# Layer 0 of a four-layer graph network: an interleaved order for its loop, and the threshold guess in two parts

## The chip, the cores and the metric

The kernel runs on one core of a Trainium2 chip. The metric is the device time in microseconds (us). A core has five engines that run their own instruction streams: TensorE (PE; its weight loads are listed as PEld), VectorE (DVE), ScalarE (ACT), GpSimd (POOL) and SyncE (SP), which issues most DMAs. Each engine works its instructions off in order; an instruction whose input is not ready holds up all that are queued behind it on that engine.

## The reference, cut to what matters

There are 4096 nodes with 256 features and a sparse adjacency `adj` (about one entry in a thousand, and the diagonal). Four layers are added to x one after the other, each on relu(layernorm(x)). The change concerns layer 0 alone:

```python
for n in range(2):
    q, k = Xa @ W1.T @ W2.T, Xa @ W3.T            # 64 features
    probs = softmax(q @ k.T)                      # 4096 x 4096
    # keep the largest probabilities of a row until their sum reaches 0.9
    A = probs * mask
    A = A / A.sum(-1)
    Xf = R @ Xf                                   # R: adj + 1, rows scaled to sum 1
    Xa = A @ Xa
    Z = Z + Xf @ U1[n].T + Xa @ U2[n].T
h = layernorm(X + Z)
```

So each of the two steps needs, for each of 4096 rows, a threshold below which its probabilities are dropped. Layers 1 to 3 (a graph convolution, graph attention, a last convolution) are not touched.

## The kernel before, in words

The rows are cut into 32 blocks of 128 (`NB`, `P`): one block is a tile `e` of 128 rows by 4096 columns. `layer0_step` (L1044) builds the functions of one step n, and `period` (L1467) issues the work of one period, b, in which several blocks are under way at once. The order of VectorE, ScalarE and TensorE is the order of the calls, since the code stands under a manual schedule of these three engines; GpSimd and SyncE are ordered by the framework. A block passes through these functions:

- `logits` (L1054) and `exponentials` (L1075): TensorE computes q times k into PSUM, ScalarE takes exp of it into `e`, with a guessed threshold of the row subtracted (`minus_guesses`), in four operations of 1024 columns; their sums give the row's total.
- the search for the threshold: `evaluate` (L1088) passes over `e` on ScalarE twice, with Sign and with Relu, shifted by the present threshold; the accumulated results are the number of entries above it and the mass above it. Points 0 and 1 use the first 1024 columns, points 2 and 3 all 4096. `aim` (L1105) sets the mass to be cut; `update` (L1142, with `measured` and `stepped`) computes the next threshold in some dozen VectorE operations on 128x1 tiles, each of which needs the one before. `bound` (L1160) does the same after point 3 with about 29 of them, and gives an upper bound `hi`.
- `below` (L1210): VectorE takes the entries under `hi` (4096 wide); `segments` (L1218): sixteen maxima (the eight largest of 256 columns each); `listing` (L1225): eleven operations on these 128 candidates, in turn the eight largest and their removal; `decide` (L1238): eight small operations choose the final threshold; `cut` (L1261) and `drop` (L1269) remove what lies under it from `e` (4096 wide each). `drop` also has three small operations for the row's scale `ra`.
- `flip`, `take`, `attend` (L1299 to L1321): TensorE transposes `e` in 8 chunks, ScalarE copies each from PSUM, TensorE multiplies by the features. `attended` (L1327), `turn` (L1338), `weighted` (L1347), `store_xa`, `store_h`, `next_keys` (L1376) finish the block in step 0: the product with U1 and U2 and the keys of step 1. Products of `weighted` and of `next_keys` share one PSUM slot. `add_heads` adds the block to the sum in step 1.
- diffusion (R times Xf): in step 0, `mark` (L1332) reduces the adjacency's rows, loaded in four pieces, to maxima of groups, four reductions a period on VectorE. From these `listed_columns` lists the columns of the entries in pairs of blocks (20 pairs). In step 1 `reach`, `mix` and `mixed` (L1389 to L1425) gather neighbours with GpSimd's indirect DMAs, sum them on TensorE and add them on VectorE, for d=0 first and d=1 later; `spread` and `finish` end a block in the second half of step 1.

`guess` (L938) computes the first thresholds of all 32 blocks from the moments of the keys: squares in eight groups of 512 nodes on TensorE and VectorE, and then a chain of 16 VectorE operations on 128x32 tiles. It runs once at the end of `front` (L983, which normalizes x and builds keys and queries) and once at the end of `close` (L1573), which finishes block 31 of step 0 and lists 14 pairs of columns. The main loops (L1631 to L1661) run periods -2 to 31 for step 0, and -2 to 33 for step 1; the last six pairs are listed in periods -2 and -1 of step 1.

In a period before the change VectorE's order is: `below`, 16 maxima, `update`(b+1, 2), `listing`, two `mark`, `store_xa`'s addition, `aim` and `update`(b+2, 0), `decide`, `cut`, `bound`(b+1), `update`(b+2, 1), two `mark`, `drop`.

## Time and profile before

| | us |
|---|---|
| median of 3 runs | 3821.71 (3820.54 to 3823.34) |
| the profiled execution | 3814.87 |
| its span | 3812.6 |
| first `below` of step 0 | 175.4 |
| last `below` of step 0 | 1441 |
| first `below` of step 1 | 1590 |
| last `below` of step 1 | 2867 |
| layers 1 to 3 begin, about | 2931 |

The mean granted TensorE clock was 0.839. In step 0 `below` comes every 40.95 us; in step 1 every 40.6 to 40.95 us in the first half and every 41.6 to 43.1 us in the second.

How such a page is read: busy time is given for each engine over the span, and in 40 slices of it (a digit is the busy tenth of a slice). Waits are listed as "engine, tile, line <- the engine, tile and line waited for: us in total, times, the longest". A windows view gives for each stretch its length and the busy time of PE, PEld, DVE, ACT and POOL. A timeline line is: start, duration, engine, line, operation, output <- inputs, shapes, how many, and in brackets the idle time before it and what ended it. L12 is line 12 of the kernel.

### The profile page before, as it was taken

What the parts mean: (1) busy time and instruction counts of PE and PEld (TensorE: products, weight loads), DVE (VectorE), ACT (ScalarE), POOL (GpSimd) and SP (SyncE); (2) the same over time, 40 slices, a digit from 0 to 9 for tenths busy, and PEclk for the clock granted to TensorE, in tenths of its full rate; (3) what the DMA queues carried; (4) which work ended last, traced back from release to release, by engine and by line L of the source; (5) the groups of instructions that cost most, each with busy time, mean ns of one, the idle gap of its engine ahead of it and who ended that gap; (6) DMA issues with size and microseconds to landing.
All of it is one profiled execution on the core that took longest, in us unless ns stands there. A gap on an engine that the chain in (4) does not pass through costs nothing. (4 is left out here: it accounts for less than half of the span.)

```text
span 3812.6 us, 43836 instructions
## 1 busy us (share of the span) xinstructions
PE 2628.0 (69%) x12404; PEld 2015.3 (53%) x12404; DVE 2878.5 (75%) x9339; ACT 2245.8 (59%) x3339; POOL 1332.3 (35%) x1342
## 2 busy tenths in 40 slices
PE   6456776776776767467767767767775657688776
PEld 5244554554554555256656656555654445577644
DVE  3499999999999998788888888888884434588500
ACT  3577777777777761676676676767661311577400
POOL 1000000000000000476666625555563476465276
PEclk8778888888888888688878878888887889789878
DMA  3012122122122121333333322222223455444375
GB/s 101 8 63 69 60 75 69 60 75 70 60 75 69 60 91 32 112 111 92 98 107 93 95 65 75 86 90 76 79 88 103 150 168 158 119 128 130 104 216 166
DMA packets 214105, 357.01 MB, mean 94 GB/s; under 512 B 34136, under 2 KB 147293, under 8 KB 213853
## 3 DMA queue, kind: packets, MB, share of 16 engines
q1 hardware_dynamic: 169356, 237.74, 19.5%
q0 software_dynamic: 43520, 116.14, 11.3%
q8 instruction: 102, 1.67, 0.2%
q14 instruction: 151, 1.23, 0.1%
q10 hardware_dynamic: 976, 0.23, 0.0%
HBM read 290.85 MB, written 63.13 MB: 93 GB/s over the span
## 5 line engine op out<-in xcount | busy, mean ns | idle before, releaser
L1096 ACT ACTIVATE unread<-e,next_pair 128x4096 uint8<-128x4096 f32 (+1 forms) x384 | 1098.5, 2861 | 368.7 <-DVE next_pair L1140 237.1
L1305 PE MATMUL pat<-ident,e 128*128 128x128 f32 x2048 | 374.7, 343 | 750.7 <-DVE ra L1274 628.1
L1305 PEld LDWEIGHTS pat<-ident,e 128*128 128x128 f32 x2048 | 306.7, 178 | 848.5 <-issue 663.2
L1321 PE MATMUL pa<-va,at 128*128 128x256 f32 x2048 | 495.0, 400 | 0.1
L1321 PE MATMUL pa<-h,at 128*128 128x256 f32 x2048 | 461.3, 381 | 0.1
L1321 PEld LDWEIGHTS pa<-va,at 128*128 128x128 f32 x2048 | 409.0, 204 | 79.9 <-issue 22.0
L1223 POOL COPY eighth<-best 128x16 f32<-128x16 f32 x64 | 16.8, 262 | 1181.0 <-DVE full_goal L1147 1180.2
L1321 PEld LDWEIGHTS pa<-h,at 128*128 128x128 f32 x2048 | 384.0, 190 | 85.4 <-issue 37.3
L1312 ACT COPY at<-pat 128x512 f32<-128x512 f32 x512 | 287.2, 589 | 142.4 <-PE pa L1321 80.0
L1080 ACT ACTIVATE e<-pl,minus_guess 128x1024 f32<-128x1024 f32 x256 | 283.2, 1114 | 137.5 <-PE pl L1066 116.3
L833 POOL DMA_INDIRECT vg<-v_d,column x320 | 307.0, 959 | 120.4 <-issue 98.3
L1222 DVE MAX8 best<-near 128x8 f32<-128x256 f32 x1024 | 340.9, 411 | 6.3
L1066 PE MATMUL pl<-kt,qb 64*128 64x512 f32 x1024 | 270.3, 638 | 94.7 <-ACT e L1080 94.7
L848 PE MATMUL acc<-vg,ac 128*128 128x256 f32 x768 | 237.9, 459 | 88.0 <-DMA vg<-v_d,column 75.9
L1265 DVE SCALAR_TENSOR_TENSOR e<-e,end_t 128x4096 f32<-128x4096 f32 x64 | 286.6, 4478 | 0.0
L1214 DVE SCALAR_TENSOR_TENSOR near<-e,end_hi 128x4096 f32<-128x4096 f32 x64 | 286.4, 4476 | 0.0
L1272 DVE MATCH_REPLACE8 e<-drop,e 128x4096 f32<-128x4096 f32 x64 | 282.2, 4409 | 0.0
L833 POOL DMA_INDIRECT vg<-far_d,column x160 | 210.0, 1313 | 129.7 <-DVE near L819 81.2
L1909 PE MATMUL acc<-u,tabg 128*65 128x128 f32 x1536 | 210.0, 293 | 61.9 <-DVE u L1894 51.2
L833 POOL DMA_INDIRECT vg<-mixed_d,column x160 | 207.5, 1297 | 125.9 <-PE pr L852 61.6
L848 PEld LDWEIGHTS acc<-vg,ac 128*128 128x128 f32 x768 | 165.7, 229 | 155.9 <-DMA vg<-v_d,column 105.0
L833 POOL DMA_INDIRECT ac<-in_adjt,adj_row x160 | 211.9, 1324 | 79.0 <-issue 40.4
(535 smaller groups left out, 4602.4 us busy)
## 6 DMA issues: line engine op xcount, KB each, us to landing
adj<-in_adjt SPq DMA_DIRECT2D x128, 512.0 KB
ac<-adjc_d SPq DMA_DIRECT2D x96, 384.0 KB
adjc_d<-ac SPq DMA_DIRECT2D x32, 384.0 KB
v_d<-v SPq DMA_DIRECT2D x64, 128.0 KB
vg<-v_d SPq DMA_DIRECT2D x64, 128.0 KB
targets<-steep_d SPq DMA_DIRECT2D x32, 256.0 KB
vg<-v_d,column POOLq DMA_INDIRECT x320, 3.8
table_d<-tab SPq DMA_DIRECT2D x32, 132.0 KB
```

The costliest lines, as they stand in the source:

```text
L833: nc.gpsimd.indirect_dma_start(out, None, rows, bass.IndirectOffsetOnAxis(ap=index, axis=0))
L848: nc.tensor.matmul(acc, ac[:, k, :], v[:, k, :], start=(k == 0), stop=(k == CHUNKS and not own))
L1066: nc.tensor.matmul(pl[:, r, :], s["qb"][rows], kt[rows, j * 512 : (j + 1) * 512], start=True, stop=True,)
L1080: nc.scalar.activation(s["e"][:, j * 1024 : (j + 1) * 1024], pl.rearrange("p r c -> p (r c)"), AF.Exp, bias=minus_guess[:, b : b + 1], acc ...
L1096: nc.scalar.activation(unread[:, :width], s["e"][:, :width], func, bias=s["at"], scale=-1.0, accum_out=s["signs"] if func == AF.Sign else ...
L1214: nc.vector.scalar_tensor_tensor(near, s["e"], end["hi"][:, b : b + 1], s["e"], op0=ALU.is_lt, op1=ALU.mult, accum_out=s["low"])
L1222: nc.vector.max(best[:, k, :], near[:, k * (N // SEG) : (k + 1) * (N // SEG)])
L1265: nc.vector.scalar_tensor_tensor(s["e"], s["e"], last, s["e"], op0=ALU.is_ge, op1=ALU.mult, accum_out=s["held"])
L1272: nc.vector.match_replace(s["e"][:, ::-1], s["drop"], s["e"][:, ::-1], 0.0)
L1305: nc.tensor.transpose(pt[:, k, :], s["e"][:, c * P : (c + 1) * P], ident)
L1312: nc.scalar.copy(at, s["pt", g])
L1321: nc.tensor.matmul(s["pa"], s["at", g][:, k, :], va[:, c, :D], start=(c == 0), stop=(c == NB - 1))
```

## The change

- `some`, `along` and `beside` are added, and the functions made of small VectorE operations become generators that give way after each operation. `along` issues one operation of each of its lines in turn; `beside` issues one of the others after each operation of the first line.
- `period` is ordered anew. The first transposes and takes of the block before, and Sign of point 3, are issued ahead of `below`. After four maxima come more transposes, takes and Relu of point 3; each further maximum is followed by an operation of `bound`. `listing`, the rest of `bound`, and `aim` with `update` 0 go in turn; so do `decide` and two of the marks; then `update` 1. `update` 2 moves from behind the next period's maxima to the end of its own period, in turn with the operations for `ra`, which leave `drop` and become `kept`.
- On ScalarE, Sign of point 2 comes directly after `update` 1, and Relu of point 2 behind the copies of the keys and of `weighted`.
- In step 0 `attended`, `turn`, `next_keys`, `weighted`, `store_xa` and `store_h` treat block b-1 in period b, where they treated b-2 (`attended` b-1).
- `bound` handles its pair of differences and its pair of sums in one operation each, instead of two; `mark` reduces halves of its columns, eight operations a period instead of four.
- `guess` is a generator in two parts: the first group of 512 nodes (blocks 0 to 3), with a chain of its own, and the other seven groups, with another. The second part is issued after period -2 of the step.
- `front` runs with a lag of six blocks instead of five, and its relu is issued one block earlier.
- `close` lists 10 pairs of columns, after period -2 of step 1 five more are listed, and after period -1 the last five.

The diff, cut to its core (of `period` the removed lines are left out, since the function before is printed above):

```diff
 
+    def some(steps, k):
+
+        for _ in zip(range(k), steps):
+            pass
+
+    def along(*lines):
+
+        lines = [iter(line) for line in lines]
+        while lines:
+            for line in list(lines):
+                try:
+                    next(line)
+                except StopIteration:
+                    lines.remove(line)
+
+    def beside(line, *others):
+
+        for _ in line:
+            for other in others:
+                next(other, None)
+
...
+        for lo, hi in ((0, 1), (1, 8)):
+            for g in range(lo, hi + 1):
...
+            bs = slice(4 * lo, 4 * hi)
+            width = 4 * (hi - lo)
+            mu, v, y, t = (sm.tile([P, NB], F32, name=f"guess_{name}", bufs=1)[:, :width] for name in "mvyt")
+            bits = sm.tile([P, NB], U32, name="guess_bits", bufs=1)[:, :width]
+            nc.vector.tensor_copy(mu, pst[:, bs, 1])
...
+            nc.vector.scalar_tensor_tensor(minus_guesses[n][:, bs], mu, -1.0, v, op0=ALU.mult, op1=ALU.subtract)
+            yield
...
-        LAG = 5
+        LAG = 6
+
+        def relu(b):
+            if b % 4 == 0:
+                group = slice(b, b + 4)
+                nc.vector.scalar_tensor_tensor(
+                    shift[:, group, 0], spread_[:, group, 0], -1.0, scale[:, group, 0], op0=ALU.mult, op1=ALU.mult
+                )
+            nc.scalar.activation(
+                h0[:, b, :], x0[b // 16][:, b % 16, :], AF.Relu, bias=shift[:, b, :], scale=scale[:, b, :]
+            )
+
...
+            if 0 <= o + 1 < NB:
+                relu(o + 1)
...
-        guess(0, pm, qt)
+        guesses = guess(0, pm, qt)
+        next(guesses)
+        return guesses
...
-            pair = s["pair"] = s["next"] if k == 3 else small("pair", 2)
+            pair = s["pair"] = s["next"] if k >= 2 else small("pair", 2)
             low, twice, steep = pair[:, 1:2], small("twice"), small("steep")
             nc.vector.tensor_scalar(twice, s["signs"], float(width), s["at"], op0=ALU.add, op1=ALU.mult)
+            yield
             nc.vector.scalar_tensor_tensor(
                 low, twice, 0.5, s["gap"], op0=ALU.mult, op1=ALU.subtract
             )
+            yield
...
+            yield from stepped(pair[:, 0:1], m, s["at"])
+            s["before"], s["next"] = s["pair"], pair
             s["at"] = pair[:, 0:1]
...
-            for k, (new, old) in enumerate(zip((t, low), s["before"])):
-                nc.vector.tensor_sub(diff[:, k : k + 1], new, old)
-                nc.vector.tensor_add(total[:, k : k + 1], new, old)
+            nc.vector.tensor_sub(diff, s["pair"], s["before"])
+            yield
+            nc.vector.tensor_add(total, s["pair"], s["before"])
+            yield
...
+            s = state[b]
+            nc.vector.match_replace(s["e"][:, ::-1], s["drop"], s["e"][:, ::-1], 0.0)
+
+        def kept(b):
+
             s, col = state[b], slice(b, b + 1)
-            nc.vector.match_replace(s["e"][:, ::-1], s["drop"], s["e"][:, ::-1], 0.0)
             ra = s["ra"] = small("ra")
             nc.vector.scalar_tensor_tensor(
                 ra, end["extra"][:, col], end["t"][:, col], s["held"], op0=ALU.mult, op1=ALU.subtract
             )
...
         def mark(b, qs):
             for q in qs:
-                nc.vector.tensor_reduce(
-                    marks[:, :, q, b], state[b]["adj"][q], AX.X, ALU.max, apply_absolute_value=True
-                )
+                for part in (slice(0, CA // 2), slice(CA // 2, CA)):
+                    nc.vector.tensor_reduce(
+                        marks[:, part, q, b],
+                        state[b]["adj"][q][:, part, :],
+                        AX.X,
+                        ALU.max,
+                        apply_absolute_value=True,
+                    )
+                    yield
...
         def period(b):
 
+            old, cur, mid, new = (0 <= k < NB for k in (b - 1, b, b + 1, b + 2))
+            opened, diffused = old and n == 0, pair(b)
             for d, k in pair(b - 1):
                 if k:
                     spread(d)
                     finish(d)
+            if n == 1 and b in (0, NB // 2):
+                reach(0, b // (NB // 2))
+                reach(1, b // (NB // 2))
+            if cur and n == 0:
+                state[b]["adj"] = load_adj(extra, b)
             if old:
                 flip(b - 1, 0)
                 flip(b - 1, 1)
                 take(b - 1, (0, 1))
+            if mid:
+                evaluate(b + 1, 3, (AF.Sign,))
+            best, order = (segments(b), listing(b)) if cur else (iter(()), iter(()))
+            if cur:
+                below(b)
+                some(best, 4)
             if old:
                 flip(b - 1, 2)
                 flip(b - 1, 3)
+                attend(b - 1, 0)
+                attend(b - 1, 1)
+                take(b - 1, (2, 3))
+            if mid:
+                evaluate(b + 1, 3, (AF.Relu,))
+            ahead = bound(b + 1) if mid else iter(())
+            beside(best, ahead)
             if new:
                 exponentials(b + 2)
             if old:
                 flip(b - 1, 4)
                 flip(b - 1, 5)
+                attend(b - 1, 2)
+                attend(b - 1, 3)
             if new:
                 logits(b + 2, 1)
             if old:
                 take(b - 1, (4, 5))
                 flip(b - 1, 6)
                 flip(b - 1, 7)
+            if new:
+                exponentials(b + 2)
+                evaluate(b + 2, 0)
             if old:
                 attend(b - 1, 4)
                 attend(b - 1, 5)
                 take(b - 1, (6, 7))
+            for d, k in diffused[:1]:
+                mix(d, k)
+            if old:
                 attend(b - 1, 6)
                 attend(b - 1, 7)
+            along(order, ahead, chain(aim(b + 2), update(b + 2, 0)) if new else iter(()))
             if new:
                 evaluate(b + 2, 1)
+            if cur:
+                along(decide(b), mark(b, (0, 1)) if n == 0 else iter(()))
+            if opened:
+                attended(b - 1)
+                turn(b - 1)
+            extras = [add_heads(b - 1)] if old and n == 1 else []
+            extras += [mixed(d, k) for d, k in diffused[:1]]
+            along(update(b + 2, 1) if new else iter(()), chain(*extras))
+            if new:
+                evaluate(b + 2, 2, (AF.Sign,))
+            if opened:
+                next_keys(b - 1)
+                weighted(b - 1, 0)
+            if cur:
+                cut(b)
+            if opened:
+                store_xa(b - 1)
+                weighted(b - 1, 1)
+            if new:
+                evaluate(b + 2, 2, (AF.Relu,))
+            if opened:
+                store_h(b - 1)
             if 0 <= b + 3 < NB:
                 logits(b + 3, 0)
             for d, k in diffused[1:]:
                 mix(d, k)
             if cur:
+                if n == 0:
+                    some(mark(b, (2, 3)), 4)
                 drop(b)
+            extras = [kept(b)] if cur else []
+            extras += [mixed(d, k) for d, k in diffused[1:]]
+            along(update(b + 2, 2) if new else iter(()), chain(*extras))
 
         def close(lists):
-
-
-            def listed(k):
-                for _ in zip(range(k), lists):
-                    pass
 
             last = NB - 1
             qt = e_pool.tile([P, N], F32, name="e")
             for g in range(3):
                 cols = slice(g * 1024, (g + 1) * 1024)
                 nc.sync.dma_start(qt[:, cols], q_d[1][:, cols])
-            listed(1)
+            some(lists, 1)
             pm = ps.tile([P, 2, 512], F32, name="pl").rearrange("p r c -> p (r c)")
-            turn(last - 1)
-            next_keys(last - 1)
             nc.sync.dma_start(qt[:, 3072 : last * P], q_d[1][:, 3072 : last * P])
             for g in range(0, 8, 2):
                 flip(last, g)
@@ -1595,26 +1678,22 @@
                     add_moments(g // 2 - 1, pm)
                 if g < 6:
                     by_node(kt1, g // 2)
-                if g == 0:
-                    weighted(last - 1, 0)
-                    store_xa(last - 1)
-                if g == 2:
-                    weighted(last - 1, 1)
-                    store_h(last - 1)
                 attend(last, g)
                 attend(last, g + 1)
             attended(last)
-            listed(14)
+            some(lists, 10)
             turn(last)
             next_keys(last, qt)
             by_node(kt1, 3)
             weighted(last, 0)
             add_moments(3, pm)
             store_xa(last)
-            guess(1, pm, qt)
+            guesses = guess(1, pm, qt)
+            next(guesses)
             weighted(last, 1)
             store_h(last)
             verify()
+            return guesses
 
         return period, logits, verify, close
 
@@ -1629,16 +1708,18 @@
             for n in range(2):
                 nc.sync.dma_start(wu[i][:, :, 1 - n, :], u[n].rearrange("(c p) m -> p c m", p=P))
         with tc.tile_pool(name="front", bufs=1) as xs, tc.manual_schedule(engines=MANUAL):
-            front(h0, kt0, xs)
+            guesses = front(h0, kt0, xs)
         own = st.enter_context(tc.tile_pool(name="own0", bufs=1))
         adj_pool = st.enter_context(tc.tile_pool(name="adj0", bufs=4))
         with tc.manual_schedule(engines=MANUAL):
             period, logits, verify, close = layer0_step(0, h0, kt0, own, adj_pool)
             logits(0, 0)
-            for b in range(-2, NB):
+            period(-2)
+            some(guesses, 2)
+            for b in range(-1, NB):
                 period(b)
             lists = listed_columns(marks, near, ps)
-            close(lists)
+            guesses = close(lists)
 
     with ExitStack() as st:
         s1 = st.enter_context(tc.tile_pool(name="s1", bufs=1))
@@ -1652,12 +1733,11 @@
             logits(0, 0)
             for b in range(-2, NB + 2):
                 period(b)
-                if b < 0:
-                    for _ in zip(range(8), lists):
-                        pass
+                if b == -2:
+                    some(guesses, 2)
+                    some(lists, 5)
                 if b == -1:
-                    for _ in lists:
-                        pass
+                    some(lists, 99)
             verify()
     layer0.close()
 
```

The generators' other functions (`aim`, `stepped`, `update`, `bound`, `segments`, `listing`, `decide`, `mixed`, `add_heads`) are changed only by a `yield` after each operation.

## Prediction

> **What bounds the kernel now.** I read the page's slices first, to see which engine fills layer 0, then the windows by period, to see whether it is full or only often busy, then the timeline of one period for the pitch (start to start) of its operations, and last the waits and the chain.
>
> ```profile
> DVE  3499999999999998788888888888884434588500
> ACT  3577777777777761676676676767661311577400
> 569.70:610.65 40.95, 28.54 (x134) 21.04 (x134) 38.29 (x125) 30.74 (x39) 0.45 (x3) 0.87 0.22 68
> 2700.00:2742.00 42.00, 30.62 (x140) 24.25 (x140) 35.77 (x128) 29.57 (x37) 23.88 (x22) 0.83 0.27 84
> PE pat L1305 <- DVE ra L1274: 628.1, 61, 16.1
> ACT unread L1096 <- DVE next_pair L1140: 237.1, 50, 8.1
> DVE rdeg L1417 <- PE pr L852: 46.9, 16, 3.2
> DMA 2%; POOL 2%; PE 1%; issue 1%; POOLq 0%; ACT 0%; DVE 0%; ACTq 0%
> ```
>
> The slices: VectorE is the full engine over both steps of layer 0 (nines, then eights). The windows (length, then busy PE, PEld, DVE, ACT, POOL): 38.29 of 40.95 us in step 0 and 35.77 of 42.00 late in step 1, ScalarE about 30. The waits: TensorE and ScalarE wait for VectorE, and VectorE hardly waits, except once per odd period of step 1's first half for the mix (46.9 us over 16). The chain covers 6% of the span only, so I don't use it.
>
> ```profile
> 610.62 0.15 DVE L1173 TENSOR_TENSOR diff<-next_pair 128x1 f32<-128x1 f32 x1
> 610.69 0.15 DVE L1174 TENSOR_TENSOR total<-next_pair 128x1 f32<-128x1 f32 x1
> ...
> 612.06 0.16 DVE L1185 TENSOR_TENSOR by<-square 128x1 f32<-128x1 f32 x1
> 612.26 0.16 DVE L1186 SCALAR_TENSOR_TENSOR by<-power,by 128x1 f32<-128x1 f32 x1
> 612.45 0.16 DVE L1187 SCALAR_TENSOR_TENSOR by<-power,by 128x1 f32<-128x1 f32 x1
> ...
> 617.21 3.71 ACT L1096 ACTIVATE unread<-e,next_pair 128x4096 uint8<-128x4096 f32 x1 [3.75 <-DVE next_pair L1140]
> ...
> 621.04 3.71 ACT L1096 ACTIVATE unread<-e,next_pair 128x4096 uint8<-128x4096 f32 x1
> ...
> 623.91 1.94 PE L1305 MATMUL pat<-ident,e 128*128 128x128 f32 x8 [11.45 <-DVE ra L1274]
> 624.19 4.47 DVE L1214 SCALAR_TENSOR_TENSOR near<-e,end_hi 128x4096 f32<-128x4096 f32 x1
> ...
> 640.81 0.37 ACT L1371 COPY hu<-pu 128x256 f32<-128x256 f32 x1 [1.52 <-PE pu L1351]
> ```
>
> Columns: start, duration, engine, line, operation. Two independent 128x1 operations (L1173, L1174) start 0.07 us apart, three that depend on each other (L1185 to L1187) 0.20 apart. A period has some 75 such chained operations: three `update` at about 1.9, `bound` 5.6, `decide` 1.83, `aim` 0.2, reciprocal sums 0.5, together 13.8 us, most of it latency and not work. The rest of VectorE's period: `below` 4.59, sixteen maxima 5.24, listing 3.79, marks 4.6, the hu addition 0.33, `cut` 4.40, `drop` 4.39: 27.3. Sum 41.1 against the measured period of 40.95.
>
> **What the Trainium skill says.** "VectorE: DVE Perf Modes", section The DRAIN you can't avoid, has the next operation start when the pipe is empty, so that dropping semaphores between chained operations gains nothing. "Perfetto Trace Analysis", section Optimizing Scalar/DVE Operations, gives some 60 ns per VectorE instruction and says the write acknowledgement overlaps the next one. The trace agrees with the second for independent small operations (0.07 pitch, 0.15 duration); the dependent pitch of 0.20 is what a chain pays beyond it, and is what interleaving can hide. "ScalarE: Activation LUTs", section What ACT_TABLE_LOAD costs, prices an ACTIVATE with a pointer bias at about 280 ns + 0.833 ns per element: 3.69 us for 4096, the trace has 3.71. "TensorE: Matmul & The Clock Gate", section Part 1, has TensorE fall to half clock after idling; here two transposes took 1.94 us after 11.45 us idle and 1.04 otherwise.
>
> **The change part by part.** Of each period b I set T=0 where `below`(b) starts; `update` 2 of block b+1 has then just ended.
>
> *VectorE's work.* Chain operations put between maxima, list steps and half marks cost 0.07 instead of 0.20. Maxima with eleven operations of `bound`: 5.24 + 11 x 0.07 = 6.0. Listing together with the rest of `bound` (18), `aim` and `update` 0: 5.9 by walking the order at 0.20 per dependent round. `decide` with four half marks 3.8 (8 x 0.20, 4 x 0.60; a half at 0.60 is an estimate: half of the 1.13 of a whole one, plus half of the 0.07 pitch). `update` 1 1.8 (alone with the turn), the other half marks 2.4, `update` 2 with the sums 2.1. With `below`, `cut`, `drop` and the addition: 35.9. The saving in work is 5 us a period.
>
> *The new waits in step 0.* Before, `update` 2 lay after the maxima, and `bound` came a whole `cut` later: Sign and Relu of the third point (3.83 + 3.88) lay beside marks, `drop`, `below`. Now `update` 2 ends a period, Sign 3 starts 0.18 later, the takes of chunks 2 and 3 stand between it and Relu 3 (to 4.83), so `low` is usable at 4.83 + 3.88 = 8.7. VectorE has done `below` and five maxima by 6.3: it waits 2.4, with the remaining maxima queued behind. Next ScalarE has 8.55 of exponentials A to 10.75, takes, exponentials B to about 14, Sign and Relu 0 at 1024 (2 x 1.26): `aim` and `update` 0 wait three times, together 2.1, with the listing queued behind them. Then Sign 2 goes 26.9 to 30.7 (`update` 1 ends 26.8), and the key copies (0.4) and weighted, which now stand behind Sign 2 and the keys' PSUM slot, come after: TensorE's 1.88 to 33.0, hu's copy 0.37; the addition that stood at 31.2 starts at 33.2 to 33.5: 2.2 of wait with marks and `drop` behind it. Waits 6.7. Period: 35.9 + 6.7 = 42.6; transposes after a longer idle time (1.94 for 1.04) delay the first takes and with them Relu 3 by a few tenths: 42.9. Against 40.95 that is +1.95, times 31: **+60**. The copies 0.4, weighted and Relu 2 (usable 37.2) beyond this lie beside `cut`, marks and `drop`. Bounds: each wait could be 0.7 less if ScalarE gets ahead, or 0.7 more: -1 to +1.3 per period.
>
> *Step 1, first half.* No marks and no hu addition, so the third wait is absent: `update` 1 ends at about 26.2 (`add_heads` waits 0.5 to 2 for the last attend on TensorE), `cut` to 30.6, `drop` to 35.0, Relu 2 usable at 34.1, `update` 2 with sums and the mix of d=1 to 37.5 to 38.8. Taken 38.0 against 40.9: -2.9, times 16: **-46**. Half of it is the 3.2 us wait for the mix of odd periods, which now comes after `drop`, far behind its matmul. *Second half*: the finish adds some five more VectorE operations and ScalarE's spread ahead of the takes; 38.6 against the 42.3 of the spacings of `below`: -3.7, times 16: **-59**. GpSimd, about 33 us of gathers a period, still fits into 38; at 36 it would not by much. SP's stores and gathers of `mixed_d` and `summed_d` are issued in the order of the mixes, which come earlier in the period than before; I cost them at nothing as GpSimd's slack of 5 us covers a late one.
>
> *Guess and front.* The first part treats four blocks instead of 32: one squares step of eight and a shorter TensorE pass, 11.5 us less ahead of the exponentials of block 0 (129.9 to about 118.4). The second part, about 16 us (as the whole guess before), falls on VectorE between `update` 2 of block 0 and its `bound`, where ScalarE's evaluations leave it some 10 of idle time. The norm's relu one block ahead takes 0 to 8 from the front loop, 4 taken. First `below` at 172 to 176 against 175.4: **-5** with period 0's fuller overlap.
>
> *Between the steps.* `close` lists 10 pairs of columns instead of 14 at 2.58 each, so the exponentials of step 1's first block come at 72 us after the last `below` instead of 98. But guess part 2 (16), the other ten pairs (25.8) and the chains then stand in series before the first `below`: 160 after the last one instead of 149; ScalarE's lead returns about 6 in the next period: **+5**, with 15 to either side, since it is the part whose order I could follow least.
>
> Sum: +60 - 46 - 59 - 5 + 5 = -45. On the profiled execution's 3814.87 (span 3812.6 and 2.3 around it) that is 3770; the runs' median lies 6.8 above that execution, so **3777**.
>
> **Rivals.**
>
> *A, the waits are hidden in both steps.* ScalarE gets ahead by its 9 us of slack, and VectorE's work alone sets the period: 36 to 37 in both. For it: ScalarE's 31.5 us are still below 36. Against it: `update` 2, Sign 3, Relu 3, `bound`, and Sign 2, Relu 2, `update` 2 form a loop, and a lead can't grow through one's own results. 31 x -4.5 and 32 x -5: 3822 - 300 = 3522 at most; with half of the waits in step 0 gone 3620 to 3690.
>
> *B, slower: the loop closes in step 1 too.* One mechanism, the wait of `bound`'s first operations for Relu 3, placed between the fourth and sixth maximum. Its price is the time by which Relu 3 ends after 6.2. In step 1 the spread or the mix's TensorE time stands ahead of takes 2 and 3, which stand ahead of Relu 3; TensorE's clock of 0.83 there leaves attends at 3.7 to 4.7 us for two, and each us of theirs arrives at VectorE through `add_heads` and then `update` 1 as well. At 40.9 and 42.3, before's own periods, step 1 gives nothing and step 0's +60 stands alone: 3822 + 60 - 5 + 5 = 3882; decided from a mean step-1 period of 39.7, 1.9 under before's mean of 41.6 (32 x -1.9 meets +60).
>
> *C, interleaving yields less.* If a chain operation behind a maximum of its own engine still pays 0.15, not 0.07, eleven plus some thirty operations lose 3 us a period, over 63 periods 189: 3777 + 189 = 3966; with half of it 3872. Against it: L1173/L1174's 0.07, and bound's operations have a whole maximum (0.33) between them, over their 0.20.
>
> *D, step 0 breaks even.* Hu's copy comes earlier than I walked (weighted before Sign 2 in effect), and step 0 is at 41: 3822 - 46 - 59 = 3717.
>
> **How the numbers follow.** What can be told from no change is 0.2%, 7.6 us. Chances: my forecast with its sizes (3730 to 3810) 0.40; D 0.13; A in its partial form 0.10; the sum near zero through smaller gains in step 1 (3814 to 3829) 0.08; B 0.19; C 0.10. Faster 0.63, same 0.08, slower 0.29. The time is the forecast's, 3777. The range for 8 in 10: 3690 to 3860. The likeliest case's own range is 3730 to 3810.
>
> **What would show it.** The spacing of `below` in step 0 at 42.6 to 43.2, and at 37.5 to 39.5 in step 1. New idle time of VectorE, by releaser ScalarE: about 2.4 ahead of `low` after the fifth maximum, 2 ahead of `twice` and `low` in the listing, 2.2 ahead of the hu addition, none there in step 1. The maxima with a chain operation between at a pitch of 0.40 (0.33 would mean that it is free, 0.53 that nothing is hidden). The first `below` at 172 to 176 us; exponentials of step 1's first block 26 us nearer to the last `below`, and its own first `below` some 10 farther. Time after layer 0 (2931 to the end) unchanged, as nothing there is touched. The forecast is wrong if step 0's spacing falls below 41 (D, A), or step 1's stays above 40 (B), or the pitch is over 0.45 (C).

## The result, and the profile after

The changed kernel takes 3835.47 us (median of 4 runs, 3832.11 to 3838.41), the kernel before 3821.12 beside it: ratio 1.0038, 95% interval 1.002 to 1.0055. It is slightly slower, where 3777 and faster was forecast; the range of 3690 to 3860 held the time, the direction was wrong.

The two profiled executions, cut at the first and last `below` of each step:

| stretch | before, us | after, us | difference | my sum |
|---|---|---|---|---|
| start to step 0's first `below` | 175.4 | 177.1 | +1.7 | -5 |
| step 0, first to last `below` | 1265.6 | 1363.3 | +97.7 | +60 |
| to step 1's first `below` | 149.0 | 169.0 | +20.0 | +5 |
| step 1, first to last `below` | 1277.0 | 1178.8 | -98.2 | -105 |
| rest | 945.6 | 947.9 | +2.3 | 0 |
| span | 3812.6 | 3836.1 | +23.5 | -45 |

Step 1 gave about what was forecast. Step 0 cost 38 us more than forecast, the stretch between the steps 15, the front 7. `below` comes every 44.3 to 44.5 us in most of step 0 (42.6 to 43.2 forecast), every 37.7 to 37.8 in most of step 1's first half and 37.5 in its second (37.5 to 39.5 forecast). One period, step 1's second, has 51.9.

VectorE's busy tenths in 40 slices, from the page of the changed kernel:

```profile
DVE  3387787778788778766888888888984434588500
```

The nines of step 0 are sevens and eights: VectorE has less to do and waits more. In the windows of one period each (step 0, step 1's first half, its second; length; busy PE, PEld, DVE, ACT, POOL; granted clock of TensorE, 1.00 being full; DMA share and GB/s):

```profile
973.72:1018.02 44.30, 30.96 (x134) 20.47 (x134) 35.28 (x126) 30.31 (x38) 0.46 (x3) 0.88 0.19 63
2039.70:2077.50 37.80, 30.16 (x142) 23.20 (x140) 31.84 (x122) 28.40 (x33) 27.25 (x22) 0.91 0.37 107
2626.00:2663.50 37.50, 30.55 (x140) 24.10 (x140) 33.32 (x126) 29.28 (x36) 21.89 (x23) 0.86 0.31 93
```

VectorE is busy 35.28 us where it was 38.29, in a longer period. The waits view says for what it waits (us in total, times, the longest):

```profile
DVE next_pair L1165 <- ACT unread L1133: 134.6, 65, 3.6
DVE hu L1468 <- ACT hu L1467: 123.2, 31, 4.4
...
DVE skip L1145 <- ACT e L1117: 52.9, 50, 6.4
DVE pair L1165 <- ACT unread L1133: 52.5, 64, 1.1
DVE twice L1163 <- ACT unread L1133: 50.9, 59, 3.9
```

The first, third, fourth and fifth line are the four waits walked in the prediction, here summed over the whole run; the second is the hu addition, once a period of step 0, 4.0 on average where 2.2 was forecast. In one period of step 0 VectorE's idle times of over 0.3 us are 1.90, 0.87, 0.62, 0.80 and 3.92, together 8.11 (6.7 forecast); without them the period has 36.2 (35.9 forecast). A period of before has 0.37 of such idle time and 40.6 without it. So the new order saved 4.4 us of work a period, and 7.7 of new waits came in. How the 3.92 arises, in the timeline of the changed kernel (start, duration, engine, line):

```profile
1044.86 3.71 ACT L1133 ACTIVATE unread<-e,next_pair 128x4096 uint8<-128x4096 f32 x1 [2.62 <-DVE next_pair L1184]
...
1048.57 0.24 ACT L1478 COPY kt<-pkq 64x128 f32<-64x128 f32 x1
1048.72 0.26 ACT L1480 COPY q<-pkq 128x128 f32<-128x128 f32 x1
...
1049.02 3.66 PE L1447 MATMUL pu<-wu,zt 128*128 128x512 f32 x4 [4.65 <-ACT q L1480]
...
1052.72 0.37 ACT L1467 COPY hu<-pu 128x256 f32<-128x256 f32 x1 [3.75 <-PE pu L1447]
...
1053.12 0.42 DVE L1468 TENSOR_TENSOR hu<-h,pu 128x256 f32<-128x256 f32 x1 [3.95 <-ACT hu L1467]
```

Sign 2 (L1133), the keys' copies, `weighted` (L1447), hu's copy and the addition (L1468) stand in a row, as walked. But `weighted` takes 3.66 us, not 1.88: TensorE had been idle for 4.65. The granted clock of that stretch in the changed kernel, and of a stretch of before with the same four matmuls and two others, from the windows views:

```profile
1049.00:1052.70 3.70, 3.66 (x4) 1.17 (x4) 0.17 (x2) 0.00 (x0) 0.00 (x0) 0.54 0.06 18
```
```profile
638.80:640.90 2.10, 1.98 (x6) 0.64 (x4) 2.01 (x6) 0.58 (x3) 0.25 (x2) 1.00 0.00 0
```

0.54 against 1.00. The guess's second part shows the same in the changed kernel, twice (end of the front, and between the steps):

```profile
1635.00:1660.00 25.00, 23.40 (x74) 16.57 (x74) 8.12 (x25) 10.49 (x9) 0.00 (x0) 0.50 0.00 1
131.00:156.00 25.00, 23.34 (x74) 16.57 (x74) 8.11 (x25) 10.43 (x9) 0.00 (x0) 0.50 0.00 1
```

From its first square to its thresholds each takes 25 us, where I put 16.

### The profile page after: what moved, and what is told of

It is laid out like the page before. It is cut to its first block, busy times and chain, and to the rows that moved or that the text cites. A ratio compares the mean times of both kernels' runs of the same rounds, so it can differ in the third digit from the quotient of the medians.

```text
span 3836.1 us, 43839 instructions
## 1 busy us (share of the span) xinstructions
PE 2717.8 (71%) x12404; PEld 1996.0 (52%) x12404; DVE 2698.8 (70%) x9371; ACT 2233.0 (58%) x3339; POOL 1301.1 (34%) x1342
## 5 line engine op out<-in xcount | busy, mean ns | idle before, releaser
L1133 ACT ACTIVATE unread<-e,next_pair 128x4096 uint8<-128x4096 f32 (+1 forms) x384 | 1097.0, 2857 | 428.4 <-DVE next_pair L1184 402.3
L1395 PE MATMUL pat<-ident,e 128*128 128x128 f32 x2048 | 340.1, 322 | 344.2 <-DVE e L1355 293.1
L1395 PEld LDWEIGHTS pat<-ident,e 128*128 128x128 f32 x2048 | 269.5, 164 | 471.3 <-DVE e L1355 229.4
L1411 PE MATMUL pa<-va,at 128*128 128x256 f32 x2048 | 486.9, 393 | 0.4 <-ACT at L1402 0.4
L1402 ACT COPY at<-pat 128x512 f32<-128x512 f32 x512 | 277.2, 585 | 220.0 <-PE pat L1395 198.2
L1294 DVE MAX8 best<-near 128x8 f32<-128x256 f32 x1024 | 390.9, 415 | 7.4 <-DVE near L1286 0.9
L1103 PE MATMUL pl<-kt,qb 64*128 64x512 f32 x1024 | 282.0, 653 | 98.6 <-ACT e L1117 98.3
L1447 PE MATMUL pu<-wu,zt 128*128 128x512 f32 x256 | 182.5, 853 | 175.7 <-ACT q L1480 145.0
L834 POOL DMA_INDIRECT ac<-in_adjt,adj_row x160 | 253.6, 1585 | 53.2 <-issue 48.5
L1989 PEld LDWEIGHTS acc<-u,tabg 128*65 128x65 f32 x1536 | 183.8, 148 | 88.7 <-DVE u L1974 76.7
```

The costliest lines, as they stand in the source:

```text
L834: nc.gpsimd.indirect_dma_start(out, None, rows, bass.IndirectOffsetOnAxis(ap=index, axis=0))
L1103: nc.tensor.matmul(pl[:, r, :], s["qb"][rows], kt[rows, j * 512 : (j + 1) * 512], start=True, stop=True,)
L1133: nc.scalar.activation(unread[:, :width], s["e"][:, :width], func, bias=s["at"], scale=-1.0, accum_out=s["signs"] if func == AF.Sign else ...
L1294: nc.vector.max(best[:, k, :], near[:, k * (N // SEG) : (k + 1) * (N // SEG)])
L1395: nc.tensor.transpose(pt[:, k, :], s["e"][:, c * P : (c + 1) * P], ident)
L1411: nc.tensor.matmul(s["pa"], s["at", g][:, k, :], va[:, c, :D], start=(c == 0), stop=(c == NB - 1))
```

## The experiments

My theory after this reading: three places lose, `weighted` (its place behind Sign 2, and TensorE's half clock there), the guess's second part, and the late lists of columns; and the interleaving gives most of its saving back because its chains start before their inputs are there. The rivals stand with each run. The first eight runs were on two chips on which the kernel before takes the same 3908 us (keys first to serial on one, the control to "chains later, with these" on the other); the last two and the first profile were on chips where it takes 3815 to 3821. In the control 1026 us lie behind the last `below`, against 948 in the first profile of the changed kernel. So totals are compared through ratios to the kernel before on the same chip, or to the control, and periods directly.

| kernel | us | ratio to before (95%) | step 0 period | step 1 halves |
|---|---|---|---|---|
| changed, control | 3939.6 | 1.0069 (1.0043 to 1.0094) | 44.4 | 37.7 to 38.3, 37.5 |
| keys first | 3829.1 | 0.9781 (0.9764 to 0.9798) | 40.3 to 40.9 | 38.0, 37.5 |
| TensorE kept busy | 3899.9 | 0.9970 (0.9959 to 0.9981) | 42.7 to 43.6 | 37.8, 37.5 |
| lists early | 3923.3 | 1.0036 (1.0019 to 1.0053) | 44.4 | 37.9, 37.5 |
| serial | 3999.8 | 1.0217 (1.0200 to 1.0235) | 45.2 | 38.3, 39.3 |
| guess whole | 3936.0 | 1.0066 (1.0044 to 1.0088) | 44.4 | 37.8, 37.5 |
| three undone | 3802.2 | 0.9732 (0.9704 to 0.9760) | 40.3 to 40.9 | 37.9, 37.5 |
| chains later, with these | 3706.6 | 0.9481 (0.9460 to 0.9502) | 38.1 to 39.5 | 36.9, 37.5 |
| chains later, alone | 3753.1 | 0.9833 (0.9811 to 0.9856) | 41.9 to 42.3 | 36.9, 37.6 |
| and add_heads late | 3554.9 | 0.9315 (0.9295 to 0.9335) | 38.2 to 39.5 | 35.0, 35.0 to 36.0 |

### The control

> The changed kernel again, as the control on the chip on which the next three run, since the first four experiments ran on a chip whose layers 1 to 3 take some 80 us longer, with the kernel before at 3908.6 there. Both theories: ratio to the kernel before 1.001 to 1.007; step 0's period 44.4, step 1's 37.7.

At 1.0069 it is slower here too; the periods are those of the first profile. Step 1's first two periods take 109.7 us together instead of 90.7, more than the 0.3% by which the ratio is above the 1.0038 of the first chip.

### Keys first

```diff
-            if new:
-                evaluate(b + 2, 2, (AF.Sign,))
             if opened:
                 next_keys(b - 1)
+            if new:
+                evaluate(b + 2, 2, (AF.Sign,))
+            if opened:
                 weighted(b - 1, 0)
```

> The changed kernel with one call moved: next_keys of the block before is issued ahead of Sign of point 2 instead of behind it. My theory: the addition of hu waits 3.9 us a period in step 0 because weighted can start only when ScalarE has copied the keys out of the shared PSUM slot, behind Sign 2, and then runs at half clock (3.66 us at a granted clock of 0.54). With the copies ahead of Sign 2, weighted lies beside Sign 2, hu's copy stands right behind Sign 2, and the wait goes: step 0's period from 44.4 to 40.4 to 40.9, Sign 2 some 0.4 later, step 1 unchanged at 37.5 to 37.8, total about 3720. Rival: ScalarE and VectorE form a closed loop anyway (Relu 2 to update 2), so that another wait comes in its place: period 42.5 to 44, total 3780 to 3825.

Step 0 went to 40.3 to 40.9, and the total is 111 us below the control. In its timeline:

```profile
891.91 3.71 ACT L1133 ACTIVATE unread<-e,next_pair 128x4096 uint8<-128x4096 f32 x1
...
892.06 3.78 PE L1447 MATMUL pu<-wu,zt 128*128 128x512 f32 x4 [0.51 <-ACT q L1480]
...
896.29 0.42 DVE L1468 TENSOR_TENSOR hu<-h,pu 128x256 f32<-128x256 f32 x1 [0.40 <-ACT hu L1467]
```

`weighted` still takes 3.78, its length at half clock, but beside Sign 2; the addition waits 0.40 instead of 3.95. In that period the four other waits have their old lengths (1.90, 0.88, 0.62 and 0.80), and no other came in. The rival falls: the loop between ScalarE and VectorE had slack.

### TensorE kept busy

```diff
-            keys(pkq, state[b]["zt"])
+            for _ in range(4 if qt is None else 1):
+                keys(pkq, state[b]["zt"])
```

> The changed kernel, in which TensorE computes the keys' products of next_keys four times over in step 0 (same result, about 3 us more of matmuls, which lie beside Sign 2). My theory: the clock, not the place alone, makes weighted 1.8 us longer than I priced it. With TensorE busy until about 30 us into the period weighted takes 1.9 instead of 3.66 us, the wait ahead of the hu addition falls from 3.9 to about 2.1, step 0's period from 44.4 to about 42.6 (what I forecast), total about 3780. Rival: weighted is long because of its reads of weights or of PSUM after the copies: 3.66 us stays, period 44.4, total 3835 or more.

```profile
980.49 1.98 PE L1447 MATMUL pu<-wu,zt 128*128 128x512 f32 x4 [0.51 <-ACT q L1481]
...
982.91 0.42 DVE L1468 TENSOR_TENSOR hu<-h,pu 128x256 f32<-128x256 f32 x1 [2.77 <-ACT hu L1467]
```

In this timeline `weighted` has the same place, but more TensorE work ahead of it, and takes 1.98 us. The hu waits of the whole run fall from the control's 123.4 to 86.5 us, step 0 (first to last `below`) from 1363.4 to 1324.1: 1.3 us a period, near the 1.8 expected, with the period at about 43.1, the 42.9 of the forecast. So of the 3.9 us, about 1.3 come from the clock, the rest from the place. The rival (reads of weights or of PSUM) falls.

### Lists early

```diff
-                    some(lists, 5)
-                if b == -1:
                     some(lists, 99)
```

> The changed kernel with all of the last ten pairs of columns listed after period -2 of step 1, none after period -1. My theory: the changed kernel lists the last pairs just ahead of step 1's first below, so that GpSimd's gathers start at 1708.6 us, 1 us before it, and the second period (51.9 us) waits 9.5 and 5 us for transfers that stand behind them. With the lists early the gathers start some 15 to 20 us earlier, the second period falls to 38 to 41, first below moves by less than 4 us, total about 3823. Rival: GpSimd is simply overloaded in these periods, and the stall moves to the third or fourth period: total within 4 us of 3835.

GpSimd's first gather, in the timeline of the control and of this run:

```profile
1709.62 1.22 POOL L834 DMA_INDIRECT vg<-far_d,column  x1 [136.13 <-DVE near L820]
```
```profile
1688.48 1.23 POOL L834 DMA_INDIRECT vg<-far_d,column  x1 [119.28 <-DVE near L820]
```

It starts 21 us earlier, released by the last list's index (L820). Step 1's first two periods fall from 71.4 and 38.3 to 56.1 and 37.1, together by 16.5. The periods behind them grew by 2.6 in all and none by more than about 0.6, so the stall did not move on, against the rival. (The total is 16.3 below the control, but part of this is a first `below` that came 4.5 earlier, which the edit doesn't explain.)

What the stall consists of is less clear. In the first profile it lies in the second period, where VectorE waits 9.5 and 5.2 us at L1516, the addition of the mix. On this chip it lies in the first period, and is made of another kind of idle time: 27 times in the control's first two periods, 38.4 us together, VectorE stands before an operation for which no other engine is named; in this run 19 times, 22.4 us. Two of them in the control:

```profile
1738.50 0.16 DVE L1184 SCALAR_TENSOR_TENSOR next_pair<-den,ones 128x1 f32<-128x1 f32 x1 [1.24 <-DVE final L1184]
...
1743.40 0.21 DVE L1268 TENSOR_SCALAR ahead<-ahead,inverse 128x1 f32<-128x1 f32 x1 [3.97 <-issue]
```

So the late lists are shown to cost about half of the stall here; what holds VectorE in it, and the other half, stay open. On the chip of the last two runs the second period takes 53.1 us with the late lists ("chains later, alone") and 34.9 with the early ones ("and add_heads late", which has other edits too): there no stall is left.

### Serial

```diff
-        lines = [iter(line) for line in lines]
-        while lines:
-            for line in list(lines):
-                try:
-                    next(line)
-                except StopIteration:
-                    lines.remove(line)
+        for line in lines:
+            for _ in line:
+                pass
```
(in `along`; `beside` likewise runs its first line alone)

> The changed kernel with the operations issued line after line instead of in turn: along and beside are plain sequences, so bound goes behind the listing, then aim and update 0, decide before the marks, update 1 and update 2 before their companions. Nothing else is changed. My theory: interleaving hides about 5 us of chain latency a period, of which the serial order gives back 2 to 4 as the waits for Relu 3 and for point 0 fall behind other work: step 1's period from 37.7 to 39.5 to 41, step 0's from 44.4 to 45 to 47, total 3900 to 3960. Rival: the gain in step 1 comes from the placement of the mix and of the evaluations, not from interleaving: step 1 stays within 0.7 of 37.7, total within 40 of 3835.

The total is 60 us above the control, and the periods of step 1 rise by only 0.6 and 1.8, of step 0 by 0.8: between the two theories. A period of step 0 has 41.1 us without waits (36.2 interleaved), but only one wait, 4.08 for hu; a period of step 1's first half 37.6 and 0.7 (32.7 and 5.1 interleaved). So the interleaving does save 4.9 us of latency a period, and more than 4 of these come back as the waits for ScalarE (four of them, 4.2 us, in step 0). It also means that most of the gain of step 1 is not the interleaving's: the first half keeps 38.3 of before's 40.9 without it, the second 39.3 of 41.6 to 43.1. For the first half the rival is right; which part of the new placement does it was not tried.

### Guess whole

```diff
-        for lo, hi in ((0, 1), (1, 8)):
+        for lo, hi in ((0, 8),):
```
(and both parts are run where the first was)

> The changed kernel with the guess in one part (all eight groups at once, at the end of front and at the end of close, as in the kernel before); the lists stay where the change put them. My theory: the second part runs on a half-clocked TensorE (granted 0.50, a group every 3.4 us instead of 1.75), so that the split makes the two guesses 33 us each instead of 20 to 22 and pays back only what lies beside ScalarE's evaluations. Undone, the first below of step 0 comes 0 to 6 us earlier than in the changed kernel, the stretch from step 0's last below to step 1's first 0 to 10 us shorter, total 5 to 16 us below the control. Rival: the early start of the first blocks is worth more than the second part costs: the total is 5 to 20 us above the control.

The first `below` came 4.9 us earlier, but with the front and the split unchanged it lies anywhere from 172.7 to 178.1 in these runs, so this is not shown to be the edit's (173.2 here). The stretch between the steps grew by 2.5; the total is 3.6 us below the control, within the intervals. Neither theory's size is shown.

Nor does the run compare the two forms at one clock. At the end of the front the whole guess ran at full clock; between the steps it began so and then fell to half, with TensorE busy in the profile all the time:

```profile
1600.00:1605.70 5.70, 5.70 (x26) 3.23 (x26) 2.24 (x4) 0.00 (x0) 0.00 (x0) 1.00 0.07 23
1605.70:1626.40 20.70, 20.70 (x62) 14.02 (x61) 3.92 (x6) 0.00 (x0) 0.00 (x0) 0.50 0.00 1
```

From its first square to its thresholds it took 29.9 us there, against 20.8 in the kernel before.

### Three undone

This run has "guess whole" and "keys first" together, with `some(lists, 14)` in `close` and the rest of the lists after period -2.

> The guess in one part, 14 pairs of columns listed in close as before and the last ones after period -2, and next_keys ahead of Sign 2. My theory: the three places where the change loses (weighted behind Sign 2, the guess's second part, the late lists) are undone, and only its gain in step 1 and a shorter step 0 remain: step 0 at 40.4 to 40.8, the stretch between the steps 145 to 155, the second period of step 1 at 38 to 42, total 3.0 to 4.0% below the kernel before. Rival: the early lists only move the stall into the stretch between the steps: 165 or more, total 2.0 to 2.7% below.

The total, 2.7% below the kernel before, fell in the rival's band. Step 0 and the second period of step 1 (38.4, after a first of 44.6) came as I expected, but the stretch between the steps stayed at 168.0. What holds it is not what the rival names, though: the whole guess ran at half clock (windows of this kernel, then of the next one, which has the same guess):

```profile
1499.50:1526.00 26.50, 26.50 (x76) 17.48 (x74) 6.01 (x8) 0.00 (x0) 0.00 (x0) 0.50 0.00 1
```
```profile
1438.00:1453.00 15.00, 15.00 (x76) 9.86 (x74) 6.01 (x8) 0.00 (x0) 0.00 (x0) 0.93 0.01 2
```

And VectorE waits 3.9 and 3.6 us for Sign and Relu of block 1's point 2 just ahead of step 1's first `below`, since `update` 2 of block 1 now stands there. The changed kernel has the same two waits (they end 144.7 and 148.5 us into its stretch); in the kernel before `update` 2 of block 1 comes after the first `below`. From its first square to its thresholds the guess took 32.9 us here and 20.8 in the kernel before; these 12.1 and the two waits are 19.6, where the stretch is 19.0 longer than before's 149.0. In the next kernel, with the same lists and the same two waits, but 20.3 us of guess, it has 154.5.

### Chains later

```diff
-            beside(best, ahead)
+            some(best, 99)
-            along(order, ahead, chain(aim(b + 2), update(b + 2, 0)) if new else iter(()))
+            along(
+                order,
+                ahead,
+                chain(repeat(None, 10), aim(b + 2), repeat(None, 5), spaced(update(b + 2, 0), 1, 5)) if new else iter(()),
+            )
```
(`spaced` gives way five more times after the first operation; this run is "three undone" with it, and with the second marks ahead of `store_xa`)

> The kernel of e6 with VectorE's chains moved behind the waits: all 16 maxima first, bound only from the listing on, aim ten rounds later and the rest of update 0 five rounds after its first operation, the second half of the marks ahead of the hu addition. Nothing is left out. My theory: of the 5 us a period that interleaving saves, 4.2 come back as four waits for ScalarE (for Relu 3, the sums, Sign 0, Relu 0), since the chains start before their inputs are there; started later they meet no wait: step 0 at 37.5 to 39, step 1 at 35 to 36.5, total 6 to 7.5% below the kernel before. Rival: ScalarE's loop from update 2 to update 2 or GpSimd's gathers (about 33 us a period) set the period: step 1 stays at 37.3 or more and step 0 at 40 or more, total within 1% of e6.

Step 0 came as expected, and a period of it has one wait of 0.70 left. Step 1's first half went to 36.9, above the expectation; its second half didn't move from 37.5, and there VectorE waits 2.83 for `pa` at `add_heads`. The total is 5.2% below the kernel before, short of the 6 to 7.5% expected. The ratio of 0.9481 is 2.6% below that of "three undone": the rival's 1% is refuted, but its floor for the second half stood. The same edit of the chains alone in the changed kernel:

> The changed kernel with nothing but VectorE's chains moved behind their inputs (all 16 maxima first, bound from the listing on, aim ten rounds later, the rest of update 0 five rounds after its first operation). Keys, guess, lists and marks stay as the change has them. My theory: the four waits of 4.2 us a period go, of which about 2 come back as latency no longer hidden: step 1's first half from 37.7 to 36.9 to 37.3, step 0 from 44.4 to 42 to 43, because weighted still stands behind Sign 2 (earlier by some 2 us, the wait for hu stays above 3), total 60 to 80 us below the control at 3939.6. Rival: the waits only move to the hu addition, and step 0 stays within 0.7 of 44.4.

The periods came in at the lower edge of what was expected (41.9 to 42.3, 36.9), and the total at 78 us, by the difference of the ratio to the 1.0038 of the first result (to the control's 1.0069 it would be 92). The hu waits stay at 126.3 us in the run: the two losses of step 0 are separate. A wait is new, for `pa` at `add_heads`; the control has at most 0.2 there in all but the last two periods. One from each half of step 1:

```profile
1902.21 0.48 DVE L1543 SCALAR_TENSOR_TENSOR t<-pa,ra,base 128x256 f32<-128x256 f32 x1 [2.83 <-PE pa L1418]
...
2530.58 0.48 DVE L1543 SCALAR_TENSOR_TENSOR t<-pa,ra,base 128x256 f32<-128x256 f32 x1 [2.82 <-PE pa L1418]
```

### add_heads late

```diff
-            extras = [add_heads(b - 1)] if old and n == 1 else []
-            extras += [mixed(d, k) for d, k in diffused[:1]]
+            extras = [mixed(d, k) for d, k in diffused[:1]]
...
-            extras = [kept(b)] if cur else []
+            extras = [add_heads(b - 1)] if old and n == 1 else []
+            extras += [kept(b)] if cur else []
```

> The kernel of e7 with step 1's add_heads moved from beside update 1 to beside update 2. My theory: the second half of step 1 keeps its 37.5 us in every version because drop, the transposes, the eight attends and add_heads ahead of update 1 form a loop (e7 waits 2.8 us for pa there); with add_heads late the second half falls to 35.3 to 36.7, the first half hardly moves, total 12 to 35 us below e7 (3706.6). Rival: GpSimd or the spread on ScalarE holds the second half: 37.3 or more, total within 8 us of e7.

Both halves of step 1 fell, the first to 34.95 against my expectation that it would hardly move, the second to between 35.0 and 36.0, and the ratio by 1.7 points, some 60 us where 12 to 35 were expected. The run before this one, on the same chip, has the wait for `pa` in both halves, at 36.9 and 37.6; here it is gone. So the loop of `drop`, transposes, attends, `add_heads` and `update` 1 had held both halves; GpSimd had not. The windows of a period of step 0, and of each half of step 1, in this kernel:

```profile
894.00:932.30 38.30, 30.03 (x134) 19.68 (x132) 36.29 (x126) 30.21 (x38) 0.46 (x3) 0.96 0.23 73
1900.00:1935.00 35.00, 30.08 (x143) 23.36 (x142) 33.12 (x122) 28.32 (x33) 25.52 (x23) 0.95 0.40 115
2400.00:2435.00 35.00, 31.16 (x140) 24.48 (x139) 32.07 (x121) 28.32 (x35) 22.18 (x22) 0.89 0.31 91
```

VectorE is again busy for 92 to 95% of the period, but the period is 2.7 to 7 us shorter than before the change. With 3554.9 us this version beats both kernels.

### The kernel before once more

> The kernel before, profiled on this chip. Both theories: its layers 1 to 3 take some 70 to 80 us longer than in the first profile (945.6 us after the last below), its periods in step 0 are the same 40.95 us. My theory also expects its first period of step 1 below 50 us, where the changed kernel has 71, since its gathers start 30 us ahead of the first below.

This run came to a chip of the first kind (3813 us, 946 behind the last `below`), so it couldn't show how the kernel before behaves on the other: its first period of step 1 took 38.98 us, but whether it would there stays open. (Its gathers start 17 us ahead of that period, not the 30 that I had expected.)

## Why the prediction was right and wrong

- *VectorE's work*: right. 35.9 forecast, 36.2 measured; 5 us saved forecast, 4.4 measured against before and 4.9 against the serial order. (In the prediction's list the term for `decide` and four half marks is 3.8, but 8 x 0.20 and 4 x 0.60 are 4.0, and 35.9 is the sum with 4.0.) Rival C, a pitch of 0.53, is out: maxima with an operation between stand mostly 0.38 to 0.40 apart, where 0.40 was forecast.

```profile
983.26 0.41 DVE L1294 MAX8 best<-near 128x8 f32<-128x256 f32 x1
983.58 0.14 DVE L1218 SCALAR_TENSOR_TENSOR power<-gap,steep 128x1 f32<-128x1 f32 x1
983.64 0.42 DVE L1294 MAX8 best<-near 128x8 f32<-128x256 f32 x1
```

- *The first four waits*: right, 4.2 measured, 4.5 forecast. Rival A, that they are hidden, did not happen.
- *The wait for hu*: the mechanism and the row were right, the size was not, and this is the step that failed: "TensorE's 1.88 to 33.0". I took 1.88 from a row of before in which the matmuls follow others; in its new place TensorE has been idle for 4.65 us, and they take 3.4 to 3.8. The Trainium skill, "TensorE: Matmul & The Clock Gate", section Part 1, has TensorE fall to half clock after idling; I applied this to the transposes only, and it holds here just as well: 0.54 of the clock was granted. The wait of 3.92 is 1.7 longer than my 2.2, where I had allowed 0.7, and makes 44.4 of 42.9: 38 us over step 0. The run with TensorE kept busy brings the term back to 1.98, and step 0 then takes 1324.1 us (1363.4 in the control, as in the first profile). That is 58.5 more than before, where my sum has 60. Rival D's order is about what "keys first" makes, and step 0 then has D's period (41 in the prediction, 40.3 to 40.9 measured).
- *Step 1*: the periods came about as forecast (37.7 to 37.8 for 38.0, 37.5 for 38.6). The sum of -98.2 for -105 has differences that cancel: the first half gave 32 for 46, the second period's stall of 14 us being all of the difference, and the second half 66 for 59. And by the serial run most of this gain is the placement's and not the interleaving's.
- *The guess*: its second part at "about 16 us (as the whole guess before)" was also priced from a row at full clock; it took 25, twice. What this cost in total no run shows: undoing the split gained nothing clear, but between the steps most of the whole guess then ran at half clock too.
- *Between the steps*: forecast +5, measured +20. The walk had 160 us for this stretch, +11, and 6 of them back in the next period. It took 169: the 9 more are as much as the guess took beyond its 16, and step 1's first period (38.8, and 39.0 before) gave nothing back. The waits for block 1's point 2, 7.5 us, were part of the walk in step 0 and left out here; so other terms of this walk were too dear by about as much, and the record does not say which. I also had the lists' time as VectorE's alone and did not follow who waits for them: GpSimd's gathers start when the last list is done, 1 us before step 1's first `below` (17 before it in the kernel before), and the stall that follows is the second period's 14 us, which is in no line of my sum.
- *Rivals*: B's mechanism (step 1 closes its loop at before's periods) did not happen, though its path through `add_heads` is the one that held step 1 at 36.9 to 37.5 in the last runs. (Its mean of 41.6 for before's step 1 is 41.2 by the profile: 1277.0 over 31 periods.) "Slower" came about with my own mechanism at larger sizes: 37.7 us in step 0 and the 15 between the steps are 53 of the 68 us by which the sum missed; the front and step 1 are 7 each, the rest 2. With step 0's alone the sum of -45 would be -7; the sign turned with the stretch between the steps. The front's 7 are hardly more than the 5.4 by which the first `below` differs between runs with the same front.

## What to carry to other kernels

A duration read from a trace holds for the state in which that row ran: before TensorE work is moved, ask whether it will follow other TensorE work, and price it at both clocks. Interleaving dependent chains saves their latency, but a chain that is started before its input is there stalls everything behind it on an in-order engine: here putting the chains some ten rounds of the interleaving later was worth 2% by itself. When a part of a change is undone to see what it cost, look whether the undone part ran as it did before. After a reorder, walk the loop over the engines from one period to the next, and look for the one operation that ties a late result to an early consumer.

## What the runs showed of the hardware

TensorE stayed at half clock through 26.5 us in which the profile has it busy all the time (granted 0.50, the guess of "three undone"), while the same 76 matmuls took 15.0 us at 0.93 in the next kernel; in "guess whole" it fell from 1.00 to 0.50 within the same work. (The profile models the ends of matmuls, so busy does not mean fully used.) The page named above has the full clock come after some 3.4 us of sustained work; the runs disagree, at least for this alternation of matmuls of 512 columns and of two, and the measurement decides. What makes it stay at half clock was not tried.
